# Two banded layers: the second layer's bias in the first layer's pass, variance preparation on ScalarE and GpSimd, one norm column of eight on GpSimd, and an order of work written out as lists

## The chip, the cores and the metric

The kernel runs on one core of one Trainium2 chip. The time is device time in microseconds (us) of one execution, the median of several. The core has five engines with a queue each, worked in order: TensorE (PE in the profile; PEld is its weight load), VectorE (DVE), ScalarE (ACT), GpSimd (POOL) and SyncE (SP), which here only issues DMA transfers. [...]

## The reference, cut to what matters

`x` is 512 x 512 x 64 floats. Two layers follow one another, each `x = x + layer(_gn(x))`. `_gn` normalises 32 groups of two channels over the whole image. The layer, for D = 64, H = 128 hidden channels and a band of 4 to each side:

```python
xn = _ln(x, norm_scale, norm_bias)
left = (xn @ Wl + bl) * mask * sigmoid(xn @ Wlg + blg)
right = (xn @ Wr + br) * mask * sigmoid(xn @ Wrg + brg)
out_gate = sigmoid(xn @ Wog + bog)
out = _banded_ingoing(left, right, WIN)   # out[i,j] = sum over |k-i| <= 4 of left[k,i] * right[k,j]
out = _ln(out, out_norm_scale, out_norm_bias) * out_gate
return out @ Wo + bo
```

`left` is needed near the diagonal alone, so each layer computes it once for nine columns a row. The bulk is `right`, the banded product, the second norm and the last product at every one of the 262,144 places.

## The kernel before, in words

**Passes.** `input_stats` reads all of `x` for the group norm of the first layer (0 to about 230 us). Then `layer(x, mid_x, ...)` runs, which writes the intermediate image `mid_x` to DRAM and sums it on the way (`sums`, on PE, first layer alone); `mid_stats` makes the second group norm's scale `ga` and shift `gb` from the sums; and `layer(mid_x, out, ...)` runs.

**Tiling.** The rows are cut into blocks of 64 that overlap by 8. Two halves of the columns lie in partitions 0 to 63 and 64 to 127. A *unit* is 8 columns of each half of a block, one tile `z` of 128 x 512; 16 units make a chunk, and a layer has 18 chunks, 288 units. In step t of the loop in `layer` the units at several stages are worked on:

- seven or more steps ahead, GpSimd applies the group norm to `z` (`affine`: `z<-z,ga` and `z<-z,gb`; VectorE does it for the first units). A list `count` gives 0 to 2 of these per step; in each fourth step the next step's are done too (`then_affine`).
- VectorE takes the layer norm's statistics of the unit (`sti<-z`); two steps ahead GpSimd centres and scales it (`z<-z,sti`, `z<-z,rs`), one step ahead PE transposes it (`banks<-ident,z`) and ScalarE keeps the result (`zT<-banks`), which also goes to DRAM as `later`.
- in its own step PE makes the right projections in two halves (`banks<-pack,zT`), ScalarE the sigmoid (`sg<-banks`), VectorE the product (`RO<-banks,sg`).
- `mix` replaces a part of `RO` by the banded product (`bank<-RO,A`), 0 to 2 such parts a step, each copied back by ScalarE (`RO<-bank`, first half) and VectorE (second half). The ten steps that have parts have 2,1,2,2,1,2,1,2,2,1 of them; the six others have none.
- an *out* follows its unit by 30 steps, when its band is done. VectorE takes statistics of it (`sto<-RO`), ScalarE norms its eight columns (`on<-RO,nm,rs`, 8 a unit), PE makes the gate from `later` (`bank<-zg,pack`) and turns `on` (`bank<-ident,on`), VectorE multiplies (`ZH<-bank,pack,gate`), PE makes the last product a step later (`bank<-pack,ZH`), and VectorE adds it to the residual tile (`XR<-bank,XR`), which is stored.
- GpSimd adds a bias row to the residual tile beforehand (`biased`: `XR<-XR,fewer` or `XR<-XR,pack`), in both layers. In the first layer it adds `bo` less a shift that keeps `mid_x` near zero mean, in the second `bo` and the shift (`shifted`, L282).

**The solve.** In each fourth step (`solve`, L598) the statistics of the units and outs that have gathered are made into inverse deviations: four small instructions on VectorE (`var<-sti`, `var<-sto,pack`, `var<-var`, `nm<-sto`), the seed of an inverse root on VectorE (`rs<-var`, integer arithmetic on the bits), then ten steps of refinement on GpSimd (`rsqrt`, L134) and two that put in the mask.

**Buffers.** `one_bank` takes from a pool of single banks (`ps`, three in the first layer, four in the second), for gates, turns, last products and the band; `two_banks` from a pool of two double banks (`ps2`), for the projections and the transposes of the units. `on` has one buffer, `XR` four, `z` twelve, `rs` three.

**Order.** Instructions go out in the order in which the loop's body (L800 to L910) calls them, on each engine (`InOrder`, L365). Every instruction recorded by that helper has line 373 in the profile, so groups are told apart by the names of their tiles. Within a step GpSimd has: centring and scaling, affines, the solve's roots, the residual's bias, the next step's affines. PE has: first half, gates, second half, turn, transposes, last product of the step before, band, sums. VectorE's share of the solve stands before both halves' products.

## Time and profile before

| | us |
|---|---|
| median of three runs | 4812.61 (4811.29 to 4815.13) |
| the profiled execution | 4808.51 |
| its span | 4806.5 |
| first layer, steady part | about 600 to 2330 |
| second layer, steady part | about 2830 to 4600 |

The stages in the page's slices of a fortieth of the span each (120 us), busy tenths: PE, VectorE, ScalarE, GpSimd, and the granted clock of PE. The statistics pass fills the first two, the two layers are the plateaus, and each begins with a ramp of 30 steps that has units but no outs, and ends with one that has outs but no units.

```profile
PE   1025799989999999999985478888888888888888
DVE  6954788888888888888867478888888888888887
ACT  0013689888888898989883268888888888888899
POOL 0035999999999999999734589999999999999964
PEclk9997999999999999999997689999999999999999
```

An instruction's group is read as: line, engine, operation, tile written, tiles read, sizes, count, total busy time and mean. A wait is read as: who waited, for whose result, total, times, longest. An instruction's duration is not what it occupies its engine for: the next may begin before the end is recorded, or some time after it.

### The profile page before, as it was taken

To read this page: it belongs to the slowest core of one execution; us is meant where nothing else is said; L and a number is where in the kernel's file an instruction comes from. 1 tells how busy PE (TensorE), PEld (TensorE's weight loads), DVE (VectorE), ACT (ScalarE), POOL (GpSimd) and SP (SyncE) were. 2 spreads that over 40 slices of the span, in tenths; PEclk is the share of its full clock that TensorE was granted. 3 is DMA by queue.
4 is the path that set the end of the run, shared out by engine and by line. 5 is a ranking of instruction groups with operands and counts; after the bars stand their busy time and mean duration, and the time that the engine had idled before them with its cause. 6 is when DMAs were issued, how large, how long until landed. Compare 5 with 4: busy or idle time off the path is not lost. (4 is left out here: it accounts for less than half of the span.)

```text
span 4806.5 us, 193543 instructions
## 1 busy us (share of the span) xinstructions
PE 3796.6 (79%) x76306; PEld 3293.0 (69%) x76306; DVE 3929.9 (82%) x9635; ACT 3708.4 (77%) x8732; POOL 3817.1 (79%) x4739
## 2 busy tenths in 40 slices
PE   1025799989999999999985478888888888888888
PEld 0024688878888887888854467777777777777775
DVE  6954788888888888888867478888888888888887
ACT  0013689888888898989883268888888888888899
POOL 0035999999999999999734589999999999999964
PEclk9997999999999999999997689999999999999999
DMA  7859677777777777777763967777777777777876
GB/s 299 336 178 108 172 212 213 215 210 215 211 209 210 211 214 212 214 212 215 199 170 100 105 168 212 216 214 209 217 213 215 213 213 218 210 216 211 222 200 179
DMA packets 1437651, 983.63 MB, mean 205 GB/s; under 512 B 167202, under 2 KB 1284424, under 8 KB 1432392
## 3 DMA queue, kind: packets, MB, share of 16 engines
q1 hardware_dynamic: 1432064, 969.75, 73.6%
q8 instruction: 604, 9.90, 0.9%
q14 instruction: 303, 2.48, 0.2%
q10 hardware_dynamic: 4680, 1.50, 0.1%
HBM read 658.42 MB, written 312.46 MB: 202 GB/s over the span
## 5 line engine op out<-in xcount | busy, mean ns | idle before, releaser
L373 ACT ACTIVATE on<-RO,nm,rs 128x128 f32<-128x128 f32 x4608 | 1927.7, 496 | 15.3 <-PE bank L373 9.9
L373 PEld LDWEIGHTS banks<-pack,zT 64*128 64x128 f32 x18576 | 1251.3, 195 | 549.5 <-ACT zT L373 288.9
L373 PE MATMUL banks<-pack,zT 64*128 64x128 f32 x18576 | 1365.6, 289 | 272.8 <-ACT zT L373 222.6
L373 DVE TENSOR_TENSOR RO<-banks,sg 128x512 f32<-128x512 f32 (+1 forms) x1188 | 795.3, 673 | 228.3 <-POOL sg L373 116.2
L373 DVE SCALAR_TENSOR_TENSOR ZH<-bank,pack,gate 128x448 f32<-128x448 f32 (+1 forms) x1152 | 741.6, 685 | 173.3 <-PE bank L373 97.3
L373 ACT ACTIVATE sg<-banks 128x512 f32<-128x512 f32 (+1 forms) x1188 | 698.0, 589 | 188.6 <-PE banks L373 188.2
L373 DVE BATCH_NORM_STATS2 sto<-RO 128x6 f32<-128x256 f32 x2304 | 800.8, 411 | 3.7
L373 POOL TENSOR_TENSOR z<-z,gb 128x512 f32<-128x512 f32 x536 | 684.8, 1278 | 42.0
L373 PE MATMUL bank<-RO,A 64*64 64x128 f32 x18432 | 706.0, 292 | 3.9 <-ACT RO L373 2.4
L373 PE MATMUL bank<-pack,ZH 128*64 128x64 f32 x18432 | 694.6, 231 | 5.0 <-ACT gate L373 4.1
L373 POOL TENSOR_TENSOR z<-z,ga 128x512 f32<-128x512 f32 x536 | 685.6, 1279 | 3.2 <-DMA z<-mid_x 1.9
L373 POOL TENSOR_TENSOR z<-z,rs 128x512 f32<-128x512 f32 x586 | 619.3, 1057 | 46.0
L373 DVE COPY RO<-bank 128x512 f32<-128x512 f32 x576 | 398.4, 692 | 310.6 <-PE bank L373 307.3
L373 PEld LDWEIGHTS bank<-pack,ZH 128*64 128x64 f32 x18432 | 612.6, 143 | 47.3 <-ACT gate L373 8.5
L373 POOL TENSOR_TENSOR z<-z,sti 128x512 f32<-128x512 f32 x586 | 627.9, 1072 | 0.0
L373 PEld LDWEIGHTS bank<-RO,A 64*64 64x64 f32 x18432 | 582.0, 142 | 43.0 <-ACT RO L373 4.1
L373 ACT ACTIVATE gate<-bank 128x448 f32<-128x448 f32 (+1 forms) x1152 | 565.8, 545 | 34.5 <-PE bank L373 32.0
L373 ACT ACTIVATE zT<-banks 128x512 f32<-128x512 f32 (+1 forms) x1084 | 463.5, 481 | 139.6 <-PE banks L373 128.9
L373 PE MATMUL bank<-zg,pack 64*128 64x448 f32 (+1 forms) x2304 | 564.3, 556 | 4.6 <-DMA zg<-later 4.6
L373 ACT COPY RO<-bank 128x512 f32<-128x512 f32 x576 | 333.2, 579 | 282.3 <-PE bank L373 282.1
L373 PE MATMUL banks<-ident,z 64*128 64x64 f32 x4336 | 254.1, 233 | 359.2 <-DVE RO L373 336.9
L373 DVE BATCH_NORM_STATS2 sti<-z 128x6 f32<-128x128 f32 x2344 | 500.5, 280 | 15.2 <-POOL z L373 14.2
(144 smaller groups left out, 3908.6 us busy)
## 6 DMA issues: line engine op xcount, KB each, us to landing
later<-zT SPq DMA_DIRECT2D x576, 256.0 KB
A<-left_of SPq DMA_DIRECT2D x1152, 128.0 KB
zg<-later SPq DMA_DIRECT2D x576, 256.0 KB
z<-in_x_dram SPq DMA_DIRECT2D x576, 128.0 KB
z<-mid_x SPq DMA_DIRECT2D x576, 128.0 KB
gn_x<-in_x_dram SPq DMA_DIRECT2D x16, 4096.0 KB
XR<-in_x_dram SPq DMA_DIRECT2D x448, 112.0 KB
mid_x<-XR SPq DMA_DIRECT2D x448, 112.0 KB
```

Of the source, the lines that this page charges most:

```text
L373: return lambda *a, **k: tc.keep_in_program_order(f(*a, **k))
```

## The change

1. **Bias.** The first layer's pass adds `bo` of both layers to the residual (`both`, `fewer`), and there is no shift any more. The second layer has no bias step. `mid_stats`, whose sums now contain the second bias, takes it out of the sums with six small operations, and adds it to the mean.
2. **Variance preparation.** Of the solve's four instructions on VectorE, `var<-sti` and `nm<-sto` go to ScalarE; `var<-sto,pack` and the addition of epsilon go to GpSimd, with 1/H put into the mask tile `m2` beforehand. The seed stays on VectorE. `solve` returns lists, and the order places their parts one by one.
3. **Norm.** In the second layer (`NV`) the last of the eight columns of an out is made by GpSimd with `tensor_scalar`.
4. **Order.** Two lists, `FIRST` and `SECOND`, hold the order of the items for the first and the second layer. `affine` is split into `scaled` and `moved`, `inner_norm` into `centred` and `rescaled`, so that other items can stand between them.
5. **Banks.** In the first layer the band takes a double bank (`APART`); in the second it takes two single ones, as before.

The core of the diff:

```diff
+APART = (False, True)
+NV = (0, 1)
+FIRST = [
+    "inner stats", "gates", "scale", ("project", 0), ("out stats", 2), "gated",
+    ("out stats", 3), ("project", 4), "turn", "centre", ("sigmoid", 0), "move",
+    "scale next", ("out stats", 99), "solve", "bias", ("solve on", "p"), ("right", 0),
+    "last product", "rescale", ("solve on", "a"), ("sigmoid", 4), ("norm", (0, 4)),
+    ("solve on", "d"), "transpose", ("roots", 2), ("right", 4), ("band", 0), "keep",
+    ("copy a", 0), ("band", 1), ("roots", 2), "sums", ("copy a", 1), ("roots", 2),
+    "norm columns", ("roots", 2), ("roots", 99), "times gate", "move next", ("copy b", 0),
+    ("copy b", 1), ("norm", (4, 8)), "end",
+]
+SECOND = [
+    ("project", 0), ("project", 4), "inner stats", "gates", ("out stats", 2),
+    ("sigmoid", 0), ("out stats", 3), ("right", 0), ("sigmoid", 4), ("out stats", 99),
+    "solve", "scale", "gated", "centre", ("solve on", "a"), "turn", ("solve on", "p"),
+    "last product", ("solve on", "d"), ("right", 4), "move", ("roots", 2), "rescale",
+    "times gate", "end", ("roots", 2), ("roots", 2), "transpose", ("norm", (0, 4)), "keep",
+    ("norm", (4, 8)), ("roots", 2), "norm columns", ("band", 0), ("copy b", 0), ("band", 1),
+    ("roots", 99), "scale next", ("copy a", 0), ("copy b", 1), ("copy a", 1), "move next",
+]
...
-    def affine(u: Unit, engine):
-
+    def scaled(u: Unit, engine):
         engine.tensor_tensor(u.z, u.z, mid(ga, JU), ALU.mult)
+
+    def moved(u: Unit, engine):
         engine.tensor_tensor(u.z, u.z, mid(gb, JU), ALU.add)
...
-    def inner_norm(u: Unit):
-        z = u.z.rearrange("p (k t) c -> p k t c", t=2)
-        m = u.mean.unsqueeze(3).broadcast_to([P, JU // 2, 2, D])
-        en.gpsimd.tensor_tensor(z, z, m, ALU.subtract)
+    def centred(u: Unit):
+        m = last(u.mean.rearrange("p k t -> p (k t)"), D)
+        en.gpsimd.tensor_tensor(u.z, u.z, m, ALU.subtract)
+
+    def rescaled(u: Unit):
         en.gpsimd.tensor_tensor(u.z, u.z, last(u.rs, D), ALU.mult)
...
-        ph = [one_bank().rearrange("i (h t j) -> i h t j", h=q, t=2) for s in range(2)]
+        if APART[0 if stats else 1]:
+            pb = [one_bank() for s in range(2)]
+        else:
+            two = two_banks()
+            pb = [two[:, s * 512 : (s + 1) * 512] for s in range(2)]
...
         if ni:
-            en.vector.tensor_scalar(
-                v[:, :ni].rearrange("p (k t) -> p k t", t=2), sti[:, : ni // 2, 2::3],
-                1.0 / D, LN_EPS, ALU.mult, ALU.add,
+            of = sti[:, : ni // 2, 2::3]
+            act.append(
+                lambda: en.scalar.activation(
+                    pairs(v[:, :ni]), of, AF.Identity, bias=ln_eps, scale=1.0 / D
+                )
             )
...
-            en.vector.scalar_tensor_tensor(
-                vo.rearrange("p (k t) -> p k t", t=2), sto[:, :, 2::3], 1.0 / H,
-                w["m2"][:, js].rearrange("p (k t) -> p k t", t=2), ALU.mult, ALU.mult,
-            )
-            en.vector.tensor_scalar(vo, vo, LN_EPS, None, ALU.add)
-            en.vector.tensor_scalar(
-                nm.rearrange("p (k t) -> p k t", t=2), sto[:, :, 1::3], -1.0, None, ALU.mult
-            )
-        rsqrt(r, v, en.vector, en.gpsimd)
+            act.append(lambda: en.scalar.mul(pairs(nm), sto[:, :, 1::3], -1.0))
+            pool += [
+                lambda: en.gpsimd.tensor_tensor(
+                    pairs(vo), sto[:, :, 2::3], pairs(w["m2"][:, js]), ALU.mult
+                ),
+                lambda: en.gpsimd.tensor_scalar(vo, vo, LN_EPS, None, ALU.add),
+            ]
+        seed, *todo = rsqrt(r, v, en.vector, en.gpsimd)
...
+            to, of = o.on[:, j, :].rearrange("p (h t) -> p h t", t=2), RO[:, :, o.c + j, :]
+            rs, nm = o.rs[:, j : j + 1], o.nm[:, j : j + 1]
+            if pool:
+                en.gpsimd.tensor_scalar(to, of, rs, nm, ALU.mult, ALU.add)
+            else:
+                en.scalar.activation(to, of, AF.Identity, bias=nm, scale=rs)
...
-        add = fewer if stats and o.blk.m < S - WIN else w["add"]
+        add = fewer if o.blk.m < S - WIN else both
         en.gpsimd.tensor_tensor(f, f, mid(add[:n], JU // 2), ALU.add)
```

`rsqrt` keeps its operations and returns them as a list. An item is carried out in step t for the same unit or out as before; `("norm", (4, 8))` makes columns 4 to 6 in the second layer and `"norm columns"` the eighth. In the lists `"roots"` with a number takes so many operations of the solve's remaining chain.

## The prediction

> **What bounds the kernel now.** First the page: four engines are each busy for 77 to 82% of the span, so the average names no bound.
>
> ```profile
> PE 3796.6 (79%) x76306; PEld 3293.0 (69%) x76306; DVE 3929.9 (82%) x9635; ACT 3708.4 (77%) x8732; POOL 3817.1 (79%) x4739
> ```
>
> Then busy time by stretch, two of the first layer and two of the second (duration; PE, weight loads, VectorE, ScalarE, GpSimd, each with its count; clock; DMA share; GB/s):
>
> ```profile
> 1000.00:1500.00 500.00, 458.37 (x9696) 405.15 (x9692) 426.45 (x1053) 447.12 (x1042) 458.78 (x552) 0.98 0.76 212
> 1500.00:2000.00 500.00, 457.04 (x9706) 403.37 (x9708) 426.71 (x1049) 443.56 (x1032) 459.09 (x552) 0.98 0.76 211
> 3000.00:3500.00 500.00, 422.93 (x8687) 371.23 (x8688) 442.23 (x1066) 436.69 (x1046) 464.43 (x557) 0.95 0.77 213
> 3500.00:4000.00 500.00, 421.79 (x8682) 370.06 (x8680) 445.28 (x1071) 442.84 (x1061) 462.06 (x564) 0.96 0.77 214
> ```
>
> A unit of the first layer is 140 matmuls (16 of them the sums), one of the second 124, so 1000 us hold 19,402/140 = 138.6 and 17,367/124 = 140.1 units: 7.215 and 7.14 us a unit. What each engine waits for in the same 1000 us (total, times, longest), GpSimd and PE, the first layer above the second:
>
> ```profile
> POOL rsqrt L373 <- DVE rs L373: 29.3, 34, 1.9
> PE banks L373 <- DVE RO L373: 63.6, 66, 2.7
> ...
> POOL rsqrt L373 <- DVE rs L373: 19.8, 26, 1.7
> PE banks L373 <- DVE RO L373: 105.5, 91, 3.9
> ```
>
> GpSimd waits for nothing else worth naming: it is occupied for 7.00 us of each unit in both layers, 97 and 98%. PE waits 83.6 and 154.2 us in all, so it needs 6.61 and 6.04 us a unit; ScalarE, by its own waits (108.9 and 119.5), 6.43 and 6.29; VectorE (141 and 107) 6.20 and 6.38. GpSimd is the bound. The order of time shows why it is occupied longer than it is busy. GpSimd (start, duration):
>
> ```profile
> 1498.82 1.27 POOL L373 TENSOR_TENSOR z<-z,ga 128x512 f32<-128x512 f32 x1
> 1500.16 1.28 POOL L373 TENSOR_TENSOR z<-z,gb 128x512 f32<-128x512 f32 x1
> 1501.41 1.19 POOL L373 TENSOR_TENSOR XR<-XR,fewer 120x512 f32<-120x512 f32 x1
> 1502.56 1.05 POOL L373 TENSOR_TENSOR z<-z,sti 128x512 f32<-128x512 f32 x1
> 1503.69 1.04 POOL L373 TENSOR_TENSOR z<-z,rs 128x512 f32<-128x512 f32 x1
> 1504.69 1.27 POOL L373 TENSOR_TENSOR z<-z,ga 128x512 f32<-128x512 f32 x1
> ...
> 1508.62 1.26 POOL L373 TENSOR_TENSOR z<-z,gb 128x512 f32<-128x512 f32 x1
> 1510.23 0.29 POOL L373 TENSOR_TENSOR rsqrt<-rs 128x64 f32<-128x64 f32 x1 [0.35 <-DVE rs L373]
> ```
>
> An instruction that needs the one just before it starts late: ga to gb is 1.34 us from start to start, sti to rs 1.13. Where it needs something else it starts early: gb to XR 1.25, rs to ga 1.00, XR to sti 1.15. So a dependent neighbour costs some 0.1 us more (medians over both layers: 1.356 against 1.233, and 1.133 against 1.00). VectorE in the same solve:
>
> ```profile
> 1507.62 0.97 DVE L373 TENSOR_SCALAR var<-sti 128x32 f32<-128x32 f32 x1
> 1508.51 0.18 DVE L373 SCALAR_TENSOR_TENSOR var<-sto,pack 128x32 f32<-128x32 f32 x1
> 1508.72 1.20 DVE L373 TENSOR_SCALAR var<-var 128x32 f32<-128x32 f32 x1
> 1509.84 0.17 DVE L373 TENSOR_SCALAR nm<-sto 128x32 f32<-128x32 f32 x1
> 1509.96 0.20 DVE L373 TENSOR_SCALAR rs<-var 128x64 int32<-128x64 int32 x1
> ```
>
> The two long ones end when a GpSimd instruction ends (z,gb at 1509.88); alone they take 0.18. VectorE is held by GpSimd here, and PE's wait for RO is the echo.
>
> **The change, GpSimd, per unit.** Five terms.
> 1. Second layer's XR add goes: -1.15 from start to start; its bias rides on the first layer's add, which has the same shape (0).
> 2. Variance preparation: two 32-column instructions per four units in both layers, nearest rows `rs<-rs,pack` 241 ns and the 32-column scalar form 264, each with a 0.08 gap: (0.32 + 0.34)/4 = +0.17. Bounds 0.12 and 0.25 (their neighbours of 24 to 48 columns).
> 3. One norm column in the second layer. Nothing like it ran here; the nearest rows are
>
> ```profile
> L373 POOL TENSOR_SCALAR rsqrt<-rsqrt 128x64 f32<-128x64 f32 x384 | 125.3, 326 | 33.6
> ...
> L373 POOL TENSOR_SCALAR rsqrt<-rsqrt 128x32 f32<-128x32 f32 x66 | 17.4, 264 | 5.8
> ```
>
> 62 ns per 32 columns, so 128 columns give 0.45. Bounds: 0.28 (a quarter of the XR add) and 0.9 (twice the estimate, since it reads pairs 480 elements apart). I take +0.45.
> 4. Neighbours. In the built order of the new kernel no z pair stands back to back in the first layer: -0.123 - 0.133 = -0.255. In the second 0.75 of the ga pairs and 0.56 of the sti pairs are parted, and two pairs of each solve's root chain: -0.167 - 0.06 = -0.23. Bounds: nothing, and these.
> 5. The wait for the seed, 0.21 and 0.14, becomes that of a seed which starts as GpSimd's last z operation ends, 0.28 a solve: 0.07. The centring with a plainer pattern: -0.015, as the rs row (1057) against the sti row (1072).
>
> First layer: 7.00 + 0.17 - 0.255 - 0.015 + 0.07 = 6.97. Second: 7.00 - 1.15 + 0.17 + 0.45 - 0.23 - 0.015 + 0.07 = 6.30.
>
> [...]
>
> **The other engines.** VectorE loses the four preparations: (75.3 + 74.0 + 29.3 + 26.0)/576 = 0.355 a unit. Its seed stays, behind a new wait for GpSimd's var pair and ScalarE's var; GpSimd has by then begun a z operation, so I take the seed as held like var<-var in the rows above, 1.0 a solve, 0.25 a unit (bounds: nothing, as its median of 0.196 before, when GpSimd mostly stood waiting for it; 0.31, as its longest case of 1.231). Behind it stand the second RO product, both ZH and the band copies, and behind those PE. 6.20 - 0.355 + 0.25 = 6.10 and 6.27. [...]
> ScalarE gains two small instructions a solve (priced by its 256-column row, 0.39: +0.2; bounds 0.1 and 0.25) and loses one column of eight in the second layer, 0.41 from start to start: 6.63 and 6.08. PE keeps its instructions: 6.61 and 6.04; the last product now stands before the transposes, which covers 1.1 us of the RO wait. The first layer's bands move from the three single banks to the two double ones, where in a unit of two bands five users share two: a bound of PE +0.5 if each second band waits for its copies, or nothing; I take nothing, since the sums and gates (0.7 each) stand between.
> DMA bytes stay; the SP queue only exchanges the output store and the zT store in the second layer, and at 0.77 busy share has room. The six operations between layers (0.2 each) add 1; the start's stores of zeros change targets only.
>
> **From engines to periods.** Nothing runs at its own need. GpSimd's work is lumpy: a solve costs 5, an affine 2.45, and units carry 0 to 3 affines. From one norm column to the next it has 2.5 us of work (centring, rescaling, column) in a unit without either, and 11 in the heaviest (two affines 4.9, centring and rescaling 2.05, the var pair 0.66, eight roots 3.0, the column). `on` has one buffer: that column must fall between one turn and the next, a window of some 6 us; before, the XR add had nearly two units. First layer: 6.97 plus 2% as before's 97 to 98% gives 7.09: -0.125 over the 240 units in its steady part (600 to 2330) = -30. Second: GpSimd 6.30 and VectorE 6.27 are level, so I take 95%, 6.65: -0.49 over 248 units (2830 to 4600) = -121. The drain at the end, bound by ScalarE (96.6 busy of 107), gains 0.3 on 20 units: -6. Sum: -30 - 121 - 6 + 1 = -156. The profiled execution took 4808.5 (span 4806.5), 4 below the median of 4812.6; from the median the sum gives 4657, and I say 4660.
>
> **Rivals.**
> - The waits vanish: periods at GpSimd's need, 6.97 and 6.30: -59 - 208 - 6 + 1, so 4541. For it: 97% now. Against it: VectorE is level. 15%.
> - The window of the column and the held seed eat most: 7.20 and 6.95, -4 - 47 - 6 = 4756. For it: PE already waits 1.1 us a unit in the second layer. 25%.
> - Slower: VectorE waits for the var pair while GpSimd still has a lump before it. At x us held per solve the second layer is 6.02 + x/4: over 7.14 from x = 4.5. With 5 it is 7.27, +32, the first layer without gain: 4845. For it: two affines and a centring (6 us) stand ahead of the pair once in four solves. Against: only then. 11%.
> - The operations are moved and nothing follows, because PE, VectorE and ScalarE form the loop: within 0.2% (10 us, about what this measurement can tell from no change). 4%.
> - The forecast, 4660, itself 4620 to 4710: 45%.
>
> Faster 85% (45 + 15 + 25), same 4%, slower 11%. The range, 4575 to 4815, leaves out half the first rival (7 or 8%), the slower case (11%) and a sliver of no change. Its lower end is a first layer at 7.00 and a second at 6.43 (-52 - 176 - 6), its upper end both layers as before.
>
> **What would show it.** Second layer: XR rows of GpSimd gone, `on<-RO,rs,nm` near 450 ns, ga to sti without a gap, units of 6.5 to 6.8. First layer: GpSimd still 97% occupied, 7.05 to 7.15. VectorE's seed near 1.1 us. Wrong if the column costs over 0.9, if VectorE's wait at the seed exceeds 2 us, or if PE waits for double banks in the first layer.

## The result, and the profile after

The changed kernel takes 4825.7 us (median of 8 runs, 4813.9 to 4845.8) against 4812.6 (8 runs) before: a ratio of 1.0027, 95% interval 1.0015 to 1.0038. It is slower, by 0.27%; the prediction said 4660, with a range that ended at 4815. The profiled execution took 4824.53 us (span 4822.6).

The page's line of busy time. All engines but PE are busy for less than before, GpSimd for 161 us less, and the kernel is not faster:

```profile
PE 3868.2 (80%) x76306; PEld 3274.2 (68%) x76306; DVE 3748.7 (78%) x9061; ACT 3685.9 (76%) x8734; POOL 3656.2 (76%) x5027
```

Busy time by stretch (columns as in the prediction: duration; PE, weight loads, VectorE, ScalarE, GpSimd; clock; DMA share; GB/s). The first layer has fewer matmuls in 500 us than before (9,385 against 9,700), the second somewhat more (8,740 to 8,912 against 8,685):

```profile
1000.00:1500.00 500.00, 455.23 (x9385) 396.22 (x9385) 391.05 (x949) 435.81 (x1041) 447.35 (x572) 0.97 0.74 204
1500.00:2000.00 500.00, 455.68 (x9384) 396.34 (x9380) 391.12 (x955) 432.57 (x1033) 446.72 (x561) 0.96 0.74 204
3000.00:3500.00 500.00, 438.93 (x8912) 367.58 (x8912) 429.46 (x1022) 437.73 (x1033) 431.74 (x610) 0.99 0.79 216
3500.00:4000.00 500.00, 433.84 (x8738) 363.79 (x8740) 425.66 (x1011) 436.02 (x1029) 427.42 (x608) 0.99 0.79 218
```

Waits of the changed kernel in 1000 us (total, times, longest), four lines of the first layer, then three of the second:

```profile
DVE rs L390 <- POOL var L390: 66.9, 31, 4.4
...
PE banks L390 <- DVE RO L390: 55.6, 44, 3.9
...
POOL XR L390 <- DMA XR<-in_x_dram: 31.5, 22, 3.1
...
POOL z L390 <- DMA z<-in_x_dram: 17.6, 12, 3.3
...
POOL var L390 <- DVE sto L390: 57.4, 31, 4.3
...
PE banks L390 <- ACT zT L390: 52.7, 52, 1.8
DVE rs L390 <- ACT var L390: 45.8, 31, 3.8
```

New in the first layer: GpSimd waits for loads, 49 us in 1000 (before: 0.2), and VectorE waits at the seed for GpSimd's pair. GpSimd waits for 72.3 us in all, so it is occupied for 927.7/133.6 = 6.94 us a unit; in the second layer for 901.4/142.0 = 6.35.

One instruction marks each unit: VectorE's addition of the last product (`XR<-bank,XR`). Its starts cut the execution into stages, and a table from them says where the time went; a "unit" is the time from the 33rd to the 241st of a layer, over 208:

| profiled execution | before | after | bias alone | old order in the first layer |
|---|---|---|---|---|
| first mark of the first layer, from the span's start | 548.7 | 526.5 | 524.1 | 526.7 |
| first to last mark, first layer | 2010.3 | 2074.2 | 2009.7 | 2024.1 |
| from there to the second layer's first | 280.5 | 280.2 | 272.7 | 277.5 |
| first to last mark, second layer | 1962.9 | 1937.6 | 1902.7 | 1938.8 |
| unit, first layer | 7.22 | 7.49 | 7.21 | 7.24 |
| unit, second layer | 7.15 | 7.04 | 6.91 | 7.05 |

(The last two columns are the experiments before_bias and t1.) After against before: -22.2 at the start, +63.9 in the first layer, -25.3 in the second, with the stretch between them +16.1 together, as the spans differ. The forecast had nothing for the start, -30 for the first layer and -127 for the second (its drain counted in), so it missed the first layer by 94 us and the second by 102.

Each unit is read from one execution, and executions scatter. The second layer's code is the same in the changed kernel and in eight of the experiments below, and its unit reads 6.99 to 7.10 in these nine profiles; a difference of 0.1 between two single profiles is no finding. The profile of before_bias is a quick one: 4715.4 us, where the median of its four runs is 4729.9.

The same intervals, folded by the 16 steps of a chunk (mean of 13 chunks, interval 0 to 15), show which steps changed. The first row of each block says how many band parts fall into an interval, and `s` a solve. In the first layer the mark has moved to the end of the step, so a step's bands count to the interval before; equal entries are to be compared, not columns.

```
first layer
  parts  before      0s   2    1    2    2s    1    2    1    2s    2    1    0    0s   0    0    0
         before     6.25 8.01 6.73 8.43 10.64 7.69 7.94 6.67  9.46 8.38 6.44 5.73 5.96 5.69 5.78 5.76
  parts  after       2s   1    2    2    1s    2    1    2    2s    1    0    0    0s   0    0    0
         after      9.12 6.46 7.62 8.17 10.14 8.72 6.46 7.63  9.95 6.50 5.40 5.46 9.49 7.03 5.91 5.70
second layer
  parts  all three   0s   2    1    2    2s    1    2    1    2s    2    1    0    0s   0    0    0
         before     6.54 7.16 6.33 7.89 11.46 7.73 7.16 6.32 10.92 8.00 6.34 5.62 5.88 5.64 5.69 5.69
         bias alone 5.99 7.16 6.38 7.83  8.03 7.02 7.16 7.00  9.14 7.20 6.35 6.12 8.16 5.60 5.70 5.70
         after      7.94 6.99 6.05 7.79  8.55 6.59 7.00 6.89  9.25 6.87 6.92 5.46 8.44 5.64 6.28 6.02
```

In the first layer the steps without a solve became faster: two parts 7.62 instead of 8.01, one 6.46 instead of 6.7, none 5.4 to 5.9 instead of 5.75. What a solve adds to its interval and the next, against the same number of parts without one, grew from 6.2 us a chunk (0.5, 2.6 + 1.0, 1.5 + 0.4, 0.2) to 14.2 (1.5, 3.7 + 1.1, 2.3, 4.0 + 1.6). Before, the two solves in steps without bands were almost free.

The time line of the changed kernel around a solve without bands (interval 12) (start, duration; idle time ahead of it and its releaser), SP, GpSimd, VectorE:

```profile
1452.86 1.05 SPq L390 DMA_DIRECT2D mid_x<-XR  x2
1454.01 1.14 SPq L390 DMA_DIRECT2D z<-in_x_dram  x2
...
1455.22 1.28 POOL L390 TENSOR_TENSOR z<-z,gb 128x512 f32<-128x512 f32 x1
1459.77 1.27 POOL L390 TENSOR_TENSOR z<-z,ga 128x512 f32<-128x512 f32 x1 [3.26 <-DMA z<-in_x_dram]
1460.99 1.17 POOL L390 TENSOR_TENSOR XR<-XR,fewer 120x512 f32<-120x512 f32 x1
1462.12 0.26 POOL L390 TENSOR_TENSOR var<-sto,pack 128x32 f32<-128x32 f32 x1
1462.47 0.29 POOL L390 TENSOR_SCALAR var<-var 128x32 f32<-128x32 f32 x1
...
1457.71 0.69 DVE L390 TENSOR_TENSOR RO<-banks,sg 128x512 f32<-128x512 f32 x1 [0.79 <-ACT sg L390]
1462.79 0.19 DVE L390 TENSOR_SCALAR rs<-var 128x64 int32<-128x64 int32 x1 [4.39 <-POOL var L390]
1462.90 0.68 DVE L390 TENSOR_TENSOR RO<-banks,sg 128x512 f32<-128x512 f32 x1
```

The load of z goes out behind the store; "scale next" (`z<-z,ga`), which the new list puts ahead of bias, pair and seed, wants that z one step after it was asked for and waits 3.26 us; the pair, VectorE's seed and the second product behind the seed are late in turn. These lines show a late load and what follows from it, and not yet that the store makes it late: in this instance the addition that the store needs had started at 1448.82, and from 1448.16 to 1451.47 SP was issuing four loads of `A`.

### The profile page after: what moved, and what is told of

Its sections match the earlier page's. It is cut to its first block, busy times and chain, and to the rows that moved or that the text cites. A ratio compares the mean times of both kernels' runs of the same rounds, so it can differ in the third digit from the quotient of the medians.

```text
span 4822.6 us, 192988 instructions
## 1 busy us (share of the span) xinstructions
PE 3868.2 (80%) x76306; PEld 3274.2 (68%) x76306; DVE 3748.7 (78%) x9061; ACT 3685.9 (76%) x8734; POOL 3656.2 (76%) x5027
## 5 line engine op out<-in xcount | busy, mean ns | idle before, releaser
L390 ACT ACTIVATE on<-RO,nm,rs 128x128 f32<-128x128 f32 x4320 | 1814.1, 498 | 33.5 <-POOL nm L390 21.8
L390 PE MATMUL banks<-pack,zT 64*128 64x128 f32 x18576 | 1299.4, 289 | 259.5 <-ACT zT L390 221.0
L390 PEld LDWEIGHTS banks<-pack,zT 64*128 64x128 f32 x18576 | 1221.8, 198 | 409.1 <-ACT zT L390 257.9
L390 PE MATMUL bank<-zg,pack 64*128 64x448 f32 (+1 forms) x2304 | 639.3, 592 | 111.7 <-DMA zg<-later 65.9
L390 PE MATMUL bank<-pack,ZH 128*64 128x64 f32 x18432 | 668.5, 226 | 43.1 <-ACT gate L390 29.9
L390 PEld LDWEIGHTS bank<-ident,on 64*128 64x128 f32 x9216 | 408.4, 139 | 199.0 <-issue 121.9
L390 PE MATMUL bank<-ident,on 64*128 64x64 f32 x9216 | 433.0, 225 | 42.6 <-ACT gate L390 27.2
L390 PE MATMUL banks<-RO,A 64*64 64x128 f32 x9216 | 332.8, 286 | 98.3 <-DVE RO L390 92.0
L390 PE MATMUL bank<-RO,A 64*64 64x128 f32 x9216 | 365.8, 283 | 47.1 <-DVE ZH L390 44.0
L390 DVE TENSOR_TENSOR XR<-bank,XR 120x512 f32<-120x512 f32 (+1 forms) x576 | 391.3, 679 | 1.8 <-PE bank L390 1.2
```

Source lines behind the costliest of these rows:

```text
L390: return lambda *a, **k: tc.keep_in_program_order(f(*a, **k))
```

## The experiments

Kernels sent together ran on one chip and share the runs of the kernel before (4806 to 4838 us by chip), so ratios are compared, not times. Units are from each one's profiled execution.

**1. Which part of the change costs what.** Kernel before with the bias change alone (`both`, `fewer`, `mid_stats` as in the diff; order, preparation, banks as before):

```diff
-            if t in outs:
+            if stats and t in outs:
                 biased(outs[t], w, stats)
```

> The kernel before with the bias change alone: the second layer has no residual addition on GpSimd any more, in its own order. GpSimd's work of the second layer falls from 7.00 to 5.85 us a unit. If GpSimd's sum was the bound of the second layer, as I predicted, the unit falls to 6.6 to 6.7 (VectorE's 6.38 at 95 to 97%) and the time by about 115 us, to 4700. If the steps are coupled, so that what GpSimd saves in the light steps is not passed on to the solve steps, the unit falls by no more than 0.35, to 6.8 to 7.05, and the time by 25 to 85 us.

Measured: 4729.9 against 4807.2, ratio 0.9839 (0.9823 to 0.9855). The second layer's unit went to 6.91, the middle of what the coupling gave and far from the 6.6 to 6.7 of a kernel bound by GpSimd's sum. GpSimd's waits in 1000 us of the second layer rose from 19.8 to 149.3, most of it here:

```profile
POOL rsqrt L361 <- DVE rs L361: 112.7, 37, 6.5
...
POOL z L361 <- DMA z<-mid_x: 34.0, 14, 4.2
```

The folded table says where: of 18.4 us less work on GpSimd in a chunk (16 x 1.15), the two solves with bands and the steps behind them (4, 5, 8, 9) gained 6.7 us; the solve of interval 12 gave back 2.3, and intervals 7 and 11 gave back 0.7 and 0.5. Intervals 1, 2, 3, 6, 10 and 13 to 15 stayed to within 0.06: there GpSimd, occupied for 98%, was not what the step waited for. Interval 15 shows it best: the GpSimd work that starts in it falls from 6.0 to 2.8 us, and it takes 5.7 us in both kernels.

The bias alone also starts the first layer 25 us earlier. The kernel before shows why, in SP's waits from 150 to 320 us:

```profile
SPq L373 <- DMA fewer<-nothing: 21.3, 1, 21.3
```

The masks of the bias row could be written only when the shift was known, after the statistics, and SP stood 21.3 us for them; without the shift the wait is not there.

Changed kernel with the old order and single banks in the first layer (`FIRST` is the old sequence of calls; the second layer as changed):

```diff
-APART = (False, True)
+APART = (True, True)
-    "inner stats", "gates", "scale", ("project", 0), ("out stats", 2), "gated",
-...
+    ("out stats", 3), "centre", "rescale", ("project", 0), ("sigmoid", 0), "gates",
+    ("project", 4), "scale", "move", ("out stats", 99), "inner stats", "solve",
+    ("solve on", "a"), ("solve on", "p"), ("solve on", "d"), ("roots", 99), "gated",
+    ("right", 0), "bias", "turn", ("sigmoid", 4), "transpose", "times gate", "scale next",
+    "move next", "last product", ("right", 4), ("band", 0), ("norm", (0, 4)), "keep",
+    "sums", ("copy a", 0), "end", ("norm", (4, 8)), "norm columns", ("band", 1),
+    ("copy b", 0), ("copy a", 1), ("copy b", 1),
```

> The first layer takes the order and the single banks of the kernel before (bias, preparation of the variances and everything else as in the changed kernel, the solve's parts one behind the other as they stood); the second layer is that of the changed kernel without changes. If the order FIRST is what costs the first layer its time, the first layer falls from 7.49 to between 7.0 and 7.25 us a unit, and the time to 4740 to 4780. If the moves of the preparation are what costs (VectorE's seed behind GpSimd's pair), the first layer stays above 7.40 whatever the order, with VectorE waiting at the seed (rs<-var) for more than 60 us in 1000.

Measured: ratio 0.9911 (0.9896 to 0.9927), first layer 7.24. With the old order GpSimd waits for no load there. So a ladder stands: bias 0.9839; with the preparation in both layers, and column and list SECOND in the second, 0.9911; with FIRST and the double banks 1.0027. The middle step takes back 0.7%, most of it in the second layer (by the marks 36 us, against 14 in the first), FIRST with its banks another 1.2%.

Preparation back on VectorE ahead of the seed, both layers:

```diff
-        return {"a": act, "p": pool, "d": [seed], "roots": todo}
+        return {"d": vec + [seed], "roots": todo}
```

> Edit: the four small instructions of the variance preparation stand on VectorE again, right ahead of the seed; order, column, bias and banks as in the changed kernel. VectorE then waits for no pair, but its short scalar operations can be held by GpSimd's running operation as before (0.97 and 1.20 us instead of 0.18). Theory H: the gain of the wait (2.2 us and more) exceeds the 1.4 to 2.4 us of the four, first layer 7.1 to 7.35, second 6.85 to 7.05, time 4730 to 4800. Theory B or C: no gain, VectorE's 0.355 us a unit come on top, time 4825 to 4900.

Measured: 0.9989 (0.9973 to 1.0006), first layer 7.53, second 6.95. The move off VectorE costs about 0.4%, in the second layer: 6.95, and 6.97 in store_prep below, lie under all nine profiles with the moved preparation. In the first layer the result says little of the wait at the seed: the wait that goes (66.9 us in 1000, 0.50 us a unit) is as long as what VectorE's own occupation gains (5.86 to 6.35 us a unit).

The column of the second layer back on ScalarE (`NV = (0, 0)`), and the other way round, the kernel of before_bias with that one column on GpSimd:

```diff
-NV = (0, 1)
+NV = (0, 0)
```

> Edit: the eighth norm column of the second layer is made by ScalarE again; nothing else. Theory C (the tie of the column to PE's turn costs the second layer): second layer falls from 7.04 to 6.7 to 6.9, time 4750 to 4790. Theory H: the column is not what costs; ScalarE gets 0.41 us a unit more and GpSimd 0.45 less, second layer 7.0 to 7.3, time 4815 to 4890. First layer unchanged at 7.49 by both.

```diff
-            en.scalar.activation(
-                o.on[:, j, :].rearrange("p (h t) -> p h t", t=2), RO[:, :, o.c + j, :],
-                AF.Identity, bias=o.nm[:, j : j + 1], scale=o.rs[:, j : j + 1],
-            )
...
+            if j >= JU - nv:
+                en.gpsimd.tensor_scalar(to, of, rs, nm, ALU.mult, ALU.add)
+            else:
+                en.scalar.activation(to, of, AF.Identity, bias=nm, scale=rs)
```

> The kernel before with the bias change and one of the second layer's eight norm columns on GpSimd; order, preparation and banks as before. In the steps without bands ScalarE is busy for more than the step's 5.69 us (7.16 us of durations, which overlap), and GpSimd waits. If ScalarE sets those steps, the column off it takes 0.2 to 0.4 from each of the six light units and the second layer goes from 6.91 to 6.75 to 6.85 (time 4690 to 4715). If GpSimd's column, at 0.45 and standing in its fixed place, holds up the turn on PE (on has one buffer), the second layer stays at 6.88 to 7.05.

Measured: without the column 1.0021 (1.0009 to 1.0033), the same as with it; in the old order, with it, 0.9921 (0.9906 to 0.9936), 0.8% worse than before_bias, the second layer at 7.11, over both of what had been expected. The waits of that second layer:

```profile
POOL on L361 <- ACT sg L361: 84.4, 35, 4.0
...
PE banks L361 <- DVE RO L361: 83.3, 97, 2.9
```

The column's own time is 450 ns, and at its fixed place GpSimd, with work behind it, stands for ScalarE for 84.4 us in 1000, 0.6 us a unit. That the place is what costs fits the two lists; the column was not moved within one list, so it is not shown.

Single banks for the bands of the first layer in the new order:

```diff
-APART = (False, True)
+APART = (True, True)
```

> Edit: the first layer's band takes two single banks again, out of three; nothing else. In the changed kernel VectorE's band copies of the first layer start when ScalarE's copy of the same double bank ends (91.5 us of waiting in 1000). Theory B: this wait goes, first layer 7.05 to 7.2, time 4720 to 4760. Theory H: the seed's wait of 2.2 us a solve stays, first layer 7.4 to 7.5, time 4800 to 4830. A third outcome: three single banks for gates, turns, last product and band are too few in this order, first layer over 7.5, time over 4830.

Measured: 1.0284 (1.0268 to 1.0300), first layer 7.94. In the new list the double banks are worth 0.46 us a unit; with single ones the copies wait for PE:

```profile
DVE RO L390 <- PE bank L390: 157.1, 124, 2.1
ACT RO L390 <- PE bank L390: 124.8, 124, 2.1
```

**2. What makes the first layer slow.** The seed behind ZH and the pair ahead of the bias, in both lists (in the first layer the roots follow in one piece):

```diff
 FIRST = [
...
+    "inner stats", "gates", "scale", ("project", 0), ("out stats", 99), "solve", "gated",
+    ("project", 4), "turn", "centre", ("sigmoid", 0), "move", ("solve on", "p"), "bias",
+    ("right", 0), "last product", "rescale", ("solve on", "a"), ("sigmoid", 4),
+    ("norm", (0, 4)), "transpose", "scale next", ("right", 4), "times gate",
+    ("solve on", "d"), ("roots", 99), ("band", 0), "keep", ("copy a", 0), ("band", 1),
...
```

> Edit: in both lists VectorE's seed stands after ZH instead of before the second RO product, GpSimd's var pair stands ahead of the bias and of the next step's affines, ScalarE's var early, and all of sto ahead of the first RO product. Nothing else changes. In the changed kernel the seed waited 2.2 us in each solve of the first layer for the var pair (66.9 us in 31 waits in 1000 us), and the first layer's unit was 7.49 us, the second's 7.04. Theory H (the held seed and what queues behind it on VectorE cost the gain): the wait falls below 0.5 us a solve, first layer 6.95 to 7.15, second 6.75 to 6.95, time 4640 to 4720. Theory B (the band in double banks costs the first layer): first layer stays at 7.35 or more, time 4780 or more. Theory C (the window of the norm column costs the second layer): second layer stays at 7.0.

Measured: 1.0018 (1.0008 to 1.0028), first layer 7.50. VectorE's wait at the seed is gone from the list and nothing is gained: others took its place.

```profile
ACT on L389 <- POOL nm L389: 64.1, 34, 4.1
...
POOL var L389 <- DVE sto L389: 42.8, 23, 3.9
```

GpSimd's waits for loads are down from 49 to 14.6 us in 1000 here, at the same unit. So late loads are not the only way in which such an order loses its time.

The residual fetched two steps ahead, right after the sums that free its buffer:

```diff
-    ("copy a", 0), ("band", 1), ("roots", 2), "sums", ("copy a", 1), ("roots", 2),
+    ("copy a", 0), ("band", 1), ("roots", 2), "sums", "fetch", ("copy a", 1), ("roots", 2),
...
+                elif name == "fetch" and t + 2 in outs:
+                    fetch(src, outs[t + 2], w, t + 2)
```

> Changed kernel, but in the first layer the residual tile is fetched two steps ahead, right after the sums have freed its buffer, so that on SP it no longer stands behind the store and the loads of z. Theory of the late load (in the light steps GpSimd stands behind the residual's load, so it enters each solve without a lead): GpSimd's wait for the load falls from 31.5 us in 1000 to below 5, and the first layer from 7.49 to 7.25 or less (time 4770 or less). Rival (in the light steps GpSimd is not what the others wait for, the loop of PE, VectorE and ScalarE is): the wait for the load goes, but comes back as a wait for another engine, and the first layer stays at 7.42 to 7.52.

Measured: 0.9976 (0.9963 to 0.9989), first layer 7.42. The wait for XR fell from 31.5 to 1.6 us in 1000, that for z rose from 17.6 to 46.3: the next load behind the store. The unit is where the rival had it, though another load's wait took the place and not another engine's.

VectorE's residual addition earlier:

```diff
-    ("solve on", "d"), "transpose", ("roots", 2), ("right", 4), ("band", 0), "keep",
+    ("solve on", "d"), "transpose", ("roots", 2), "end", ("right", 4), ("band", 0), "keep",
...
-    ("copy b", 1), ("norm", (4, 8)), "end",
+    ("copy b", 1), ("norm", (4, 8)),
```

> Changed kernel, but in the first layer VectorE's addition of the last product to the residual (XR<-bank,XR, with its store) stands ahead of the second half's product, no longer behind the band copies and the norm. Theory of the late load: the store leaves some 2 us earlier in each step, with it the next residual load; GpSimd's wait for the load falls by half at least (31.5 to 15 or less) and the first layer to 7.3 or less. If the loop of PE, VectorE and ScalarE sets the time: VectorE now holds the second product up, the first layer stays at 7.45 to 7.6.

Measured: 1.0129 (1.0110 to 1.0148), first layer 7.65, over both expectations. Loads are less late (24 us instead of 49), but VectorE stands ahead of the second product for PE's last product:

```profile
DVE XR L390 <- PE bank L390: 67.6, 79, 1.2
```

The store behind the next step's loads on SP, and nothing else:

```diff
             if t + 2 in outs:
                 recall(outs[t + 2])
+            if stats and t - 2 in outs:
+                stored(dst, outs[t - 2])
...
                     ended(dst, p)
+                    if not stats or t == last_t + 2:
+                        stored(dst, p)
```

(`stored` holds the two DMA issues that stood at the end of `ended`.)

> Changed kernel, but in the first layer the output store of a step is issued on SP behind the next step's loads of z and of the residual, no longer ahead of them; nothing else moves. Theory of the late load: in the changed kernel every load of the first layer stands on SP behind a store that waits for the last instruction of VectorE's step, so GpSimd gets z and XR late (31.5 and 17.6 us waited in 1000), and its var pair, VectorE's seed and PE behind it are late in turn. Then GpSimd's two waits fall below 10 us together, VectorE's wait at the seed from 66.9 to below 35, and the first layer from 7.49 to 7.30 or less (time 4770 or less). Rival (it is the place of the work in the list, not the load): GpSimd's waits for DMA go, another wait takes their place, and the first layer stays at 7.40 to 7.52.

Measured: 0.9952 (0.9936 to 0.9969), first layer 7.34, between the two expectations. Of the 0.0116 between t1 and the changed kernel 0.0075 come back from the place of one DMA issue: the late store is a cause, and not all of it. The gain lies in the solves with bands, intervals 4 and 8, which go from 10.14 and 9.95 to 9.13 and 9.32; interval 12, whose time line stands above, doesn't gain (9.83 after 9.49). First layer:

```profile
DVE rs L390 <- POOL var L390: 38.9, 27, 4.2
...
POOL XR L390 <- DMA XR<-in_x_dram: 16.2, 10, 3.6
...
POOL z L390 <- DMA z<-in_x_dram: 11.3, 10, 1.8
...
SPq L390 <- DMA mid_x<-XR: 65.8, 73, 2.9
```

The last line says that the queue still isn't free: the fetch now waits for a store of its buffer to land, as there are four buffers.

"Scale next" behind the roots, alone and with the store behind the loads:

```diff
-    "scale next", ("out stats", 99), "solve", "bias", ("solve on", "p"), ("right", 0),
+    ("out stats", 99), "solve", "bias", ("solve on", "p"), ("right", 0),
-    "norm columns", ("roots", 2), ("roots", 99), "times gate", "move next", ("copy b", 0),
+    "norm columns", ("roots", 2), ("roots", 99), "times gate", "scale next", "move next", ("copy b", 0),
```

> Changed kernel, but in the first layer the multiplication of the next step's affine (scale next, the z,ga whose load came 3.26 us late in the solve step without bands) stands behind the roots, no longer ahead of bias, var pair and seed. Theory of the chain load, z,ga, XR, var pair, seed, second product, ZH, PE: VectorE's wait at the seed falls from 66.9 to below 40 and the solve steps without bands (unit 12 of 16, 9.5) to 7.5 or less; the first layer to 7.25 to 7.38. Rival (a solve step takes its 9 to 10 us from its own work, in whatever order): unit 12 stays above 8.5 and the first layer at 7.42 to 7.52.

> Both edits of the two runs before: the first layer's store behind the next loads, and the next affine's multiplication behind the roots. If each takes away a part of the same chain, the two together reach the first layer of the kernel before or less, 7.10 to 7.25 (time 4725 to 4765); if one of the two is the cause and the other nothing, the better of the two runs comes out again within 0.03.

Measured: alone 0.9988 (0.9976 to 1.0000), first layer 7.46, interval 12 still 9.72: it missed what the chain theory gave and came out at the rival's figures; GpSimd's next operation, the bias, then waits for its load (48.8 us in 1000). Together 0.9921 (0.9892 to 0.9949), first layer 7.32, interval 12 at 9.13 (6.22 with the old order). The ratio is near the 0.9911 of the old order, but its interval is wide, and it overlaps that of the store alone. By the marks of the profiles the two edits bring back 38 of the 50 us that FIRST costs the first layer (2074.2 to 2036.1, old order 2024.1), the store alone 33 (2041.3). With 7.34 and 7.32 within 0.03, the second of the two expectations came true: that "scale next" adds anything to the store is not shown.

The fetch after the sums and the store behind the loads, both diffs together:

> Changed kernel, in the first layer with the store behind the next loads, and the residual fetched two steps ahead, right after the sums. Theory of the late load in full (GpSimd's need of 6.94 to 7.03 plus its waits is the first layer's unit, and the loads make most of the waits): the waits of GpSimd for DMA fall from 27.5 in 1000 (store behind the loads alone) to below 8 and the first layer from 7.34 to 7.15 to 7.25, time 4745 to 4765. Rival (what is left of the loss is the list's order on the other engines): the waits for DMA go and waits for VectorE or PE take their place, first layer 7.30 to 7.38, time 4775 to 4795.

Measured: 1.0424 (1.0387 to 1.0462), first layer 8.27. This was a bad experiment. The fetch, two steps ahead with four buffers, has to wait for the store that I had just put off, SP stands for it, and the loads of z behind it came later than ever:

```profile
SPq L390 <- DMA mid_x<-XR: 198.5, 152, 3.6
...
POOL z L390 <- DMA z<-in_x_dram: 98.8, 31, 7.1
```

It doesn't tell the two theories apart, but it is the dose in the other direction: 135 us of GpSimd's waits for loads (PE waits for loads too, 46.3 us), and 0.79 us more a unit. More buffers would have been the clean test; it was not run.

The diffs of store_after and prep_vector together:

> Changed kernel with the first layer's store behind the next loads and the whole preparation of the variances back on VectorE ahead of the seed (both layers). If the loss of the first layer has two shares, the late loads and VectorE's wait at the seed for GpSimd's pair, the two edits together bring it from 7.49 to 7.20 to 7.28, and with a second layer at 6.95 the time to about 4735 to 4755. If the wait at the seed is only an echo of GpSimd's lag, which the late loads make and the order of the list keeps, the first layer stays where the store alone brought it, 7.32 to 7.40, and the time at 4765 to 4785.

Measured: 0.9927 (0.9904 to 0.9950), first layer 7.32, second 6.97. VectorE waits for no pair at the seed any more, and the first layer stands where the store alone had brought it. That is what the echo was to give, but it doesn't settle it: with the store moved, the wait at the seed was 0.29 us a unit (38.9 us in 1000), and VectorE's own occupation grew by 0.31 (5.94 to 6.25), so a gain and a cost of one size would look the same. For the echo speaks t1, where VectorE waits 39.2 us in 1000 at the seed and the unit is 7.24.

**3. Was GpSimd the bound of the first layer?** The kernel of before_bias with GpSimd's z operations parted, in both layers and in the first alone (`inner_norm` then only centres; `some` are the step's affines on GpSimd):

```diff
             for u in inputs(t + 2):
                 inner_norm(u)
+            for u in some:
+                scaled(u, en.gpsimd)
+            for u in inputs(t + 2):
+                rescaled(u)
+            for u in some:
+                moved(u, en.gpsimd)
```

> The kernel before with the bias change, and GpSimd's four z operations of a step's first part parted (centre, scale, rescale, move instead of centre, rescale, scale, move); no other engine's order changes. As I predicted, a parted pair saves 0.12 to 0.13 us. If GpSimd's sum is the bound of the first layer (it waits for 27 us in 1000 only), its need falls by 0.1 to 0.2 and the first layer goes from 7.21 to 7.02 to 7.12, the second stays within 0.05 of 6.91; time 4700 to 4710. If the other engines' loop sets the first layer as well, the first layer stays at 7.17 to 7.24 and GpSimd's waits grow by 10 to 25 us in 1000.

> The kernel before with the bias change, and GpSimd's z operations parted in the first layer alone. In the first layer GpSimd's sum is the bound (7.02 occupied of 7.21; parted in both layers it gave 7.12), in the second the parting made the loads of z late (65 us waited) and cost 0.07. Expected: first layer 7.08 to 7.15, second 6.88 to 6.95, ratio to the kernel before 0.977 to 0.983. If the second layer's 6.98 was only scatter from one execution to the next, the ratio stays at 0.982 to 0.985, as with the bias change alone or with both layers parted.

Measured: 0.9818 (0.9802 to 0.9835) and 0.9817 (0.9803 to 0.9832); first layer 7.12 and 7.15, second 6.98 and 6.97. GpSimd is occupied for 6.86 to 6.87 us a unit of the first layer instead of 7.02: a parted pair does save what the starts had shown, and in these profiles about half of it reaches the unit. In the first layer it is the solves that gain, as in the second above: parted in both layers, intervals 4, 5 and 8 go from 10.72, 7.50 and 9.37 to 9.97, 7.36 and 9.11, and interval 0 from 6.42 to 6.06, while those in steps with no solve near them stay to within 0.03. Whether the second layer is parted makes no difference to it, and not parted, with the code of before_bias, it reads 6.97: the 6.91 above was a quick execution. Both ratios' intervals overlap that of the bias alone, so the times don't show the gain.

The store behind the loads in the kernel of before_bias, in both layers, alone and with the parting:

```diff
+            if t - 2 in outs:
+                stored(dst, outs[t - 2])
```

> The kernel before with the bias change, and the output store behind the next step's loads on SP in both layers. In the second layer GpSimd waits for 34 us in 1000 for z, and PE for 48 for zg; in the first layer it waits for no load. If these waits are on the path, the second layer falls from 6.91 to 6.75 to 6.85 and the time to 4690 to 4715, with the first layer unchanged (7.18 to 7.24). If they only fill time in which GpSimd and PE have nothing to do, nothing changes: 4720 to 4735.

> Both edits of the two runs before on the kernel before with the bias change. If each works in its own layer, the gains add up: 4670 to 4700. If the one layer's loop and the other's are set by PE, VectorE and ScalarE, 4720 to 4735 again.

Measured: 1.0010 (1.0000 to 1.0019) and 1.0006 (0.9994 to 1.0017): the 1.6% of the bias change are lost, which neither expectation had. SP in the second layer:

```profile
SPq L361 <- DMA out_dram<-XR: 74.0, 99, 2.5
```

Here no store had been in the way (in the second layer of before_bias SP stands 1.8 us in 1000 for `XR`), and now the fetch that must wait for the late store is. The edit that cures one order harms the other.

**The best version** of the runs is the bias change with parted z operations, 0.9818 of the kernel before; the bias alone, with 0.9839, has an interval that overlaps with it.

## Why the prediction was wrong

- *GpSimd's terms* were right: occupied for 6.94 and 6.35 us a unit against 6.97 and 6.30 forecast. The column:

```profile
L390 POOL TENSOR_SCALAR on<-RO,rs,nm 128x128 f32<-128x128 f32 x288 | 129.7, 450 | 122.8 <-ACT gate L390 118.6 <-PE bank L390 3.7
```

The 450 ns lie on the line through the rows of 32 and 64 columns (264 and 326 ns, 62 more for each 32 columns). The upper bound of 0.9 was there because the column reads pairs 480 elements apart; the 450 ns show no such cost.
- *The seed held by GpSimd, 1.0 a solve*, was wrong in the first layer and too high in the second: in the steady first layer all 57 seeds took 0.20 us, in the second 36 of 60 took over 0.25 and 17 over 0.9, mean of all 0.64. In the first layer the seed starts when the pair ends (1462.79) and GpSimd's next z operation after it (1462.84). In the second it is mostly ScalarE's `var` that ends the wait, and GpSimd has gone on by then; each of the 36 ends within 0.1 us after a z operation that had started before it, as here:

```profile
3510.12 1.27 POOL L390 TENSOR_TENSOR z<-z,gb 128x512 f32<-128x512 f32 x1
3510.19 1.26 DVE L390 TENSOR_SCALAR rs<-var 128x64 int32<-128x64 int32 x1 [0.28 <-ACT var L390]
```

At the start of the other 24 no GpSimd operation was running, and they took 0.20 us, as the seeds of the first layer did, where the z operation began 0.05 us after the seed. So in this trace a seed's length went by which of the two had started first, and the prediction had GpSimd first every time.
- *Bands in double banks, priced at nothing with a bound of +0.5*: in this order they are worth 0.46 us a unit (single_banks), a gain where the prediction had nothing or a loss. No run has them in the old order.
- *The start, priced at nothing*: -22.2 us. The wait of SP for `fewer<-nothing` stood in the trace of before; the prediction did not read SP's waits.
- *The SP queue "has room"*: this is the first step that failed. The DMA share, which the prediction went by, did not show the wait in the queue: in the first layer it is 0.76 before and 0.74 after, while SP's wait for `XR` rose from 8.2 to 54.2 us in 1000. FIRST puts VectorE's residual addition last, so the store waits on SP, and GpSimd's loads wait behind. SP's waits in 1000 us of the first layer, before and after:

```profile
SPq L373 <- DVE XR L373: 8.2, 13, 1.4
...
SPq L390 <- DVE XR L390: 54.2, 33, 3.3
```

The place of the store is 0.75 of the 1.2% (store_after). At the same time "scale next" moved forward in the step; both together are 1.1 by the ratio, 38 of 50 us by the marks, and the rest of FIRST's cost, interval 12 above all, has no cause shown.
- *"From engines to periods"* is the step that weighs most and failed in both layers: 7.09 and 6.65 forecast, 7.49 and 7.04 measured, with GpSimd's needs as forecast; with the old order in the first layer, where no load is late, it is still 7.24 and 7.05 (t1). GpSimd's 97 to 98% was the occupation of an engine with a backlog. It made the others wait in the solves with bands; in the rest the other engines must set the time, and which of them does is not shown. The folded table of before hints at it already: intervals 1 and 6 of the second layer, both with two parts, take 7.16 each, those without parts or solve 5.6 to 5.7, and before_bias, with 1.15 us a unit less on GpSimd, leaves them there. Taking the smaller of before and bias alone for each interval of the second layer, the mean is 6.69, and with the changed kernel's entries 6.59: 6.65 needed nearly every step at its best at once. A term off GpSimd was worth what the solve steps were late, not its sum: 1.15 us gave 0.18 to 0.24 (6.97 and 6.91 against 7.15), 0.155 gave 0.07 to 0.09.
- *The rivals.* "Column and held seed eat most" (4756) had the column right and the seed wrong, and the order of the first layer was in none of its terms. The slower rival (4845) had the right wait, VectorE at the seed for the pair behind GpSimd's lump, and a number near the result; but it put it in the second layer (6.02 there is VectorE's 6.38 less 0.355) at 4.5 us a solve or more, where the wait is for ScalarE's `var` and about 1.3 us a solve (45.8 us over 142/4 solves). In the first it is 2.0 us a solve on average (66.9 us over 133.6/4 solves), right at the prediction's own sign of being wrong, and taking it away gave nothing (seed_late; prep_vector and store_prep put as much work in its place).
- *What stays open*: why interval 12 of the first layer takes 9 to 10 us in the order FIRST wherever the store and "scale next" stand (the profiles of store_next and t1 are as near as they are, 4 us, because the second layer, of one code, is 8.5 us shorter in the former's); whether the wait at the seed is an echo; and what, besides the preparation's 0.4%, takes the other half of the middle step's 0.7%.

## What to carry to other kernels

Fold the step times by the pattern of the loop before adding up an engine: a step whose time was the same with and without a part of that engine's work (interval 15 of the second layer, 5.7 us with 6.0 and with 2.8 us of GpSimd's work) gained nothing when work was taken off it, though GpSimd was occupied for 98%. Read the waits of the queue that issues DMAs as those of an engine, and for each moved item ask which loads are issued behind it and who needs them first. A place in an order has a price of its own: the same column cost nothing in one list and 0.8% in another, and the same shift of a store gave 0.75% in one, in one layer, and took 1.7% in the other, in both.

## What was not expected of the hardware

- A load that waits for a buffer to be stored holds up the loads behind it on SP: SP stands 65.8 us in 1000 with the store put off, 198.5 with the fetch put ahead of it as well, and there GpSimd waits 98.8 us for `z`.
- GpSimd's dependent neighbours: parting them took 0.155 us of occupation from each unit of the first layer, in line with the starts (0.12 to 0.13 for each pair).
- GpSimd's `tensor_scalar` over 128 elements in pairs 480 elements apart took 450 ns, as much as the line through the rows of 32 and 64 columns (264 and 326 ns) gives for its length.
